# An adjacency-masked attention layer on one core: the first two graphs by rows, bias squares later, one watch operation, the last store behind the flag

## The chip, the core and the metric

The kernel runs on one core of one Trainium2 chip. The core has five engines that run side by side and wait for one another through semaphores: PE (TensorE, matrix products), DVE (VectorE), ACT (ScalarE), POOL (GpSimd) and SP (SyncE, which here only issues transfers). Data lie in HBM, on the chip in SBUF (128 partitions), and the results of PE in eight PSUM banks. The metric is the device time of one execution in microseconds (us); lower is better.

## The reference

128 graphs of 128 nodes with 768 features go through one layer: normalisation of every row, Relu, projections to queries, keys and values, attention in 12 heads of 64 with a bias and a mask from the adjacency matrix, and the sum with the input.

```python
h = jnp.maximum(_layernorm(x, axis=-1), 0.0)
q = _split_heads(h @ Wq + bq)
k = _split_heads(h @ Wk + bk)
v = _split_heads(h @ Wv + bv)
scores = jnp.einsum('bhqd,bhkd->bhqk', q, k) / jnp.sqrt(jnp.asarray(HD, x.dtype))
scores = scores + beta * adj[:, None, :, :]
scores = jnp.where(adj[:, None, :, :] > 0, scores, -9000000000000000.0)
probs = jax.nn.softmax(scores, axis=-1)
out = jnp.einsum('bhqk,bhkd->bhqd', probs, v)
return x + out.transpose(0, 2, 1, 3).reshape(B, N, D)
```

All is float32.

## The kernel before

The graphs are taken in 32 groups of four. A group's activations are held transposed, features on the partitions, as six tiles A00 to A12: A{r}{k} holds feature part k (of three) of the two graphs of half r. The products with the weights are done in three slices, `qk0`, `v` and `qk1` (the two halves of query and key columns, and the values). In most slices 18 block products are replaced by the 15 of the table `PRODUCTS`, over sums of activations (`SUMS_A`, tiles S) and of weight blocks (`SUMS_B`, tiles T). `product` (L313 on) issues the matmuls of one of them at L331, and its results are added up by ACT (L352, the first use) and DVE (L342, L347, L356). The exception is slice `qk0` of group 0: `plain_slice` takes the 18 products as they are, at L481, because the sums are not ready at the start. Its steps are counted 0 to 17, in order of r, then j (output block), then k.

The order in which things are issued is written by hand: a slice runs through its products, and behind product n it issues what the dictionary `todo` has under n (`then(n, f)`). A scheduler then places every engine's instructions in a fixed order; `tc.issue_after(i)` keeps an instruction behind another.

The start of before, for group 0. `load_x` brings each graph in four pieces of 32 rows, laid out in blocks (partition a * 32 + i holds features 192 a to 192 a + 191 of rows i, 32 + i and so on), on SP's and ACT's queues in turn. DVE takes the statistics of each block (`stats`, L227). A row's moments lie in four partitions, so PE adds them with the small matrix `mean8` (`moments_1`, L238, and `moments_2`, L254); DVE finishes them (L241 to L259), POOL raises to the power -0.5 (L261) and makes the shift (L263), ACT normalises with Relu (`norm`, L272), and DVE transposes in 32x32 blocks (`to_hT`, L279). `half(0, step)` does this for graphs 0 and 1, `half(1, step)` for graphs 2 and 3, whose moments are issued behind steps 1 and 2 of the plain slice. Ten matmuls on the identity (L530) stand behind the square matmuls of the moments, to keep PE at work. The other groups' rows are prepared in the same way during the group before, in slice v.

Attention of one output block is `scores` (L377, then DVE at L381 and ACT's exponential at L384) and `attend` (L410): products with the values, which carry a column of ones so that column HD holds the sum of the weights. `weigh` (L387 on) bounds that sum from below (L389), takes the reciprocal (L391), multiplies (L393 on DVE, L396 on ACT in group 0) and folds both the sums and the reciprocals into the running maximum `seen`, in two operations (L399). The last blocks of the last group are taken in halves, `scores_half` and `attend_half`, whose multiply, addition (L452) and store (L454) follow each other.

The adjacency bias is prepared by `bias_1` (transposed at L298, mask at L300, scaled and capped at L301, merged into `biasT` at L304); its square is taken by ACT at L305, and `bias_2` folds the largest into `seen_b` (L310, L311).

At the end DVE takes the maximum of `seen` and `seen_b` (L628, L629), tests them (L631, L632), PE adds the tests over the partitions (L634), and DVE writes the flag `bad` (L636, L637). Every engine loads the flag (L57); if it is set, the loop `general` does the whole work again in a slower and safer way (L58). With the inputs of the reference it isn't set.

SP's queue holds nearly all transfers in one order. A transfer takes one of eight slots, and one that finds its slot in use waits for the landing of the transfer before it there.

Of the kernel before, what the change touches and what calls it, by code (L numbers as in the profile page):

```python
# [10 lines left out]
F32 = mybir.dt.float32  # L11
# [85 lines left out]
HOME = {"B00": "T12", "B10": "T10", "B02": "T0", "B20": "T4", "B11": "T13"}  # L97
SLICES = ("qk0", "v", "qk1")
# [3 lines left out]
AV_AT = (5, 8, 11)  # L102

# [8 lines left out]
def direct(ctx, tc, x, adj, wq, bq, wk, bk, wv, bv, beta, out, bad):  # L112
# [41 lines left out]
    for g in range(GRP):  # L154
        load_x(0, g, (nc.sync, nc.scalar))
    ident = const.tile([P, P], F32, name="ident")
    make_identity(nc, ident)


    fold = const.tile([P, SQ], F32, name="fold")  # L160
    nc.vector.tensor_reduce(fold, ident.rearrange("p (a i) -> p i a", i=SQ), AX.X, ALU.add)
    mean8 = const.tile([P, NB, SQ], F32, name="mean8")
    made = nc.vector.tensor_scalar(mean8, fold[:, None, :].to_broadcast([P, NB, SQ]), -0.125, None, op0=ALU.mult)
# [5 lines left out]
    seen = const.tile([P, 2, 2 * GRP], F32, name="seen")  # L169
    nc.gpsimd.memset(seen, 0.0)  # L170
    seen_b = const.tile([P, GRP], F32, name="seen_b")
    nc.gpsimd.memset(seen_b, 0.0)
    vring = [const.tile([P, 2 * GRP, VE], F32, name=f"v{i}") for i in range(7)]
    for v in vring:
        nc.gpsimd.memset(v[:, :, HD:VE], 1.0)
# [16 lines left out]
    def load_weights(sl):  # L192
        for b in [f"B{k}{j}" for j in range(3) for k in range(3)]:
            t = const.tile([P, 2, H2], F32, name=f"{sl}_{HOME.get(b, b)}")
            load_block(sl, int(b[1]), int(b[2]), t)
            wt[sl, b] = t
# [12 lines left out]
    load_weights("qk0")  # L209
    beta_c = const.tile([P, 1], F32, name="beta_c")  # L210
    nc.scalar.dma_start(beta_c, beta[None, :].to_broadcast([P, 1]))

    nc.gpsimd.tensor_scalar(beta_c, beta_c, ISCALE, None, op0=ALU.mult)
# [34 lines left out]
    squares = {}  # L248

    def moments_2(G, lo, hi, mean, d):  # L250

        n = hi - lo
        for q in range(0, P, HD):
            squares[0] = nc.tensor.matmul(pm[G, lo][q:q + HD, 1], mean8.rearrange("p a i -> p (a i)")[:, q:q + HD],  # L254
                                          d, start=True, stop=True)
# [40 lines left out]
    def bias_1(G, raw):  # L296
# [8 lines left out]
        nc.scalar.activation(a, a, AF.Square)  # L305
        return a

    def bias_2(G, a):
        bm = stat.tile([P, GRP], F32, tag="bm", name=f"bm_{G}", bufs=1)
        nc.vector.tensor_reduce(bm, a, AX.X, ALU.max)  # L310
        nc.vector.tensor_tensor(seen_b, seen_b, bm, ALU.max)  # L311
# [48 lines left out]
    es, xo, taken = {}, {}, {}  # L360
# [25 lines left out]
    def weigh(G, oc, r, pa, o):  # L386

        sm = stat.tile([P, 4, 1], F32, tag="sm", name=f"sm_{G}_{oc}_{r}")
        nc.vector.tensor_scalar(sm, pa[:, :, HD:VE], TINY, None, op0=ALU.max)  # L389
        rs = stat.tile([P, 4, 1], F32, tag="rs", name=f"rs_{G}_{oc}_{r}")  # L390
        nc.vector.reciprocal(rs, sm)  # L391
        if G:
            nc.vector.tensor_mul(o, pa[:, :, 0:HD], rs.to_broadcast([P, 4, HD]))  # L393
        else:
            for b in range(4):
                nc.scalar.activation(o[:, b], pa[:, b, 0:HD], AF.Copy, scale=rs[:, b])  # L396
        for i, t in enumerate((sm, rs)):
            s = seen[:, i, 4 * r:4 * r + 4]
            nc.vector.tensor_tensor(s, s, t.rearrange("p b e -> p (b e)"), ALU.max)  # L399

    def attend(G, oc):
        o = work.tile([P, 2, 4, HD], F32, tag="o", name=f"o_{G}_{oc}", bufs=2)
        for r in range(2):
# [8 lines left out]
            weigh(G, oc, r, pa, o[:, r])  # L412
# [26 lines left out]
    def attend_half(G, oc, r):  # L439
# [9 lines left out]
        weigh(G, oc, r, pa, o)  # L449
        give(bank)  # L450
        t = xo[G, oc, r]
        nc.vector.tensor_add(t, t, o.rearrange("p (b j) d -> p b (j d)", j=2))  # L452
        g0 = G * GRP + 2 * r
        nc.sync.dma_start(out[g0:g0 + 2, :, oc * P:(oc + 1) * P].rearrange("g n d -> n g d"), t)  # L454
# [15 lines left out]
    def plain_slice(G, sl, todo):  # L470

        n = 0
        for r in range(2):
            for j in range(3):
                bank = take()
                p = bank.rearrange("p (i w) -> p i w", i=2)
                for k in range(3):
                    a, b = A[G, f"A{r}{k}"], wt[sl, f"B{k}{j}"]
                    for i in range(2):
                        for c in range(2):  # L480
                            nc.tensor.matmul(p[:, i, :], b[:, c, i * P:(i + 1) * P], a[:, c, :],  # L481
                                             start=(k == 0 and i == 0 and c == 0), stop=(c == 1),
                                             skip_group_check=True)
# [13 lines left out]
    load_weights("v")  # L497

# [269 lines left out]
```

## Time and profile before

| | us |
|---|---|
| median of 6 runs | 2901.37 |
| lowest and highest | 2899.60 and 2901.92 |
| the profiled execution | 2902.34 |
| its span, first to last instruction | 2900.1 |

| stage of group 0 and the end, by PE's lines | start, us |
|---|---|
| warm-up matmuls, L530 | 9.51 |
| plain slice, L481 | 15.84 |
| slice v, L331 | 50.9 |
| first scores, L377 | 81.4 |
| second scores, L377 | 115.9 |
| last flag operation, L637 | 2894.89 |

"Busy" is the time in which an engine had an instruction in work; PE's instructions overlap, so its records are longer than the distance from one to the next. A float32 matmul shows as two records. A line such as L481 is that of the kernel's text above; an arrow `a<-b` names the tile that is written and those that are read, without numbers. The chain of waits is followed back from the last instruction to what released it. Idle time of an engine that isn't on that chain costs nothing by itself.

### The profile page before, as it was taken

The page shows a single profiled execution, that of the slowest core. Times are in us where ns is not written, and L with a number is a line of the kernel's source. Part 1 is how long each engine was busy: PE and PEld are TensorE (multiplying, and loading weights), DVE is VectorE, ACT ScalarE, POOL GpSimd, SP SyncE. Part 2 cuts the span into 40 slices and gives each one's busy share as a digit, 9 for nine tenths or more (in the row PEclk, how much of TensorE's full clock was granted, in tenths as well). Part 3 has the DMA queues.
Part 4 walks back from the last instruction along what each step waited for, and adds up shares of the span by engine and source line. Part 5 has one row for each costly group of instructions (what it writes and reads, how often), then busy time and mean ns, then how long its engine had stood idle before and what let it go on. Part 6 is the DMA issues. An engine that isn't in the chain of part 4 may idle for free.

```text
span 2900.1 us, 81826 instructions
## 1 busy us (share of the span) xinstructions
PE 2880.3 (99%) x35526; PEld 2017.6 (70%) x35526; DVE 1985.1 (68%) x5143; ACT 804.7 (28%) x1751; POOL 375.7 (13%) x307
## 2 busy tenths in 40 slices
PE   8999999999999999999999999999999999999998
PEld 6666677667776666766667666677676677666766
DVE  6976677766676766776667676667766677666765
ACT  1432322323222222223232232322323222322221
POOL 1111111111111111111111111111111111111110
PEclk9999999999999999999999999999999999999999
DMA  6312122121222111221112212122221222111211
GB/s 162 76 53 57 41 67 71 53 61 37 63 71 60 56 44 54 71 63 52 52 46 70 71 49 59 42 63 70 56 60 39 59 71 63 52 49 45 67 42 39
DMA packets 358621, 172.21 MB, mean 59 GB/s; under 512 B 84464, under 2 KB 358128, under 8 KB 358256
## 3 DMA queue, kind: packets, MB, share of 16 engines
q1 hardware_dynamic: 355392, 166.14, 20.9%
q8 instruction: 280, 4.59, 0.6%
q10 hardware_dynamic: 2864, 0.79, 0.1%
q14 instruction: 85, 0.70, 0.1%
HBM read 116.53 MB, written 50.33 MB: 58 GB/s over the span
## 4 chain that ended last, share of the span: by engine, by line
PE 97%; DVE 1%; issue 1%; DMA 0%; POOL 0%; ACT 0%; ACTq 0%; SPq 0%; DVEq 0%; POOLq 0%
PE bank L331 83%; PE bank L377 6%; PE bank L410 6%; PE bank L481 1%; DMA x<-in_x_dram 0%; DVE A L279 0%; DVE qk L356 0%; DVE S L285 0%; POOL rstd L261 0%; DVE e L381 0%; PE bank L238 0%; PE bank L254 0%; ACT x L272 0%; DVE qk_T L207 0%; PE bank L430 0%
## 5 line engine op out<-in xcount | busy, mean ns | idle before, releaser
L331 PE MATMUL bank<-S,qk_T 128*64 128x256 f32 x7056 | 822.6, 380 | 0.5 <-DVE qk L356 0.5
L331 PEld LDWEIGHTS bank<-S,qk_T 128*64 128x64 f32 x7056 | 502.5, 137 | 257.7 <-ACT e L384 3.8
L356 DVE TENSOR_TENSOR qk<-qk,bank 128x512 f32<-128x512 f32 x630 | 429.3, 682 | 344.2 <-PE bank L331 344.0
L352 ACT ACTIVATE qk<-bank,bqk 128x256 f32<-128x256 f32 x756 | 313.0, 471 | 1020.7 <-PE bank L331 769.8
L331 PE MATMUL bank<-S,qk_B 128*64 128x256 f32 x4032 | 478.2, 379 | 1.2 <-DVE qk L356 0.9
L331 PE MATMUL bank<-A,qk_T 128*64 128x256 f32 x4032 | 478.5, 379 | 0.4 <-DVE qk L356 0.4
L415 POOL TENSOR_TENSOR xo<-xo,o 128x512 f32<-128x512 f32 x189 | 255.9, 1354 | 1601.0 <-DVE o L393 872.1
L347 DVE TENSOR_TENSOR v<-v,bank 128x512 f32<-128x512 f32 x320 | 220.2, 688 | 296.9 <-PE bank L331 296.8
L331 PE MATMUL bank<-v_T,S 128*64 128x256 f32 x3584 | 422.7, 380 | 0.0
L384 ACT ACTIVATE e<-e 128x512 f32<-128x512 f32 x378 | 227.6, 632 | 651.0 <-DVE e L381 650.3
L331 PEld LDWEIGHTS bank<-A,qk_T 128*64 128x64 f32 x4032 | 283.6, 137 | 137.6 <-DVE qk L356 0.5
L331 PEld LDWEIGHTS bank<-S,qk_B 128*64 128x64 f32 x4032 | 278.0, 137 | 129.7 <-DVE qk L356 1.4
L331 PEld LDWEIGHTS bank<-v_T,S 128*64 128x64 f32 x3584 | 252.2, 137 | 126.4 <-issue 5.7
L272 ACT ACTIVATE x<-x,shift,rstd 128x192 f32<-128x192 f32 x512 | 228.2, 536 | 344.0 <-POOL shift L263 344.0
L381 DVE SCALAR_TENSOR_TENSOR e<-bank,biasT 128x512 f32<-128x512 f32 x378 | 231.6, 682 | 20.5 <-PE bank L377 20.1
L331 PE MATMUL bank<-v_B,S 128*64 128x256 f32 x2048 | 244.7, 380 | 0.0
L331 PE MATMUL bank<-v_T,A 128*64 128x256 f32 x2048 | 238.3, 379 | 0.0
L410 PEld LDWEIGHTS bank<-v,e 128*64 128x64 f32 x6048 | 208.6, 138 | 27.4
L279 DVE STREAM_TRANSPOSE A<-x 128x256 f32<-128x256 f32 x384 | 215.3, 611 | 7.5 <-ACT x L272 7.4
L342 DVE TENSOR_TENSOR v<-bv_b,bank 128x512 f32<-128x512 f32 x192 | 131.9, 687 | 114.2 <-PE bank L331 114.2
L410 PE MATMUL bank<-v,e 128*64 128x65 f32 x6048 | 208.2, 221 | 0.0
L331 PEld LDWEIGHTS bank<-v_T,A 128*64 128x64 f32 x2048 | 147.4, 137 | 73.9
(80 smaller groups left out, 1743.4 us busy)
## 6 DMA issues: line engine op xcount, KB each, us to landing
x<-in_x_dram SPq DMA_DIRECT2D x504, 96.0 KB, 2.4
xo<-in_x_dram SPq DMA_DIRECT2D x189, 256.0 KB, 2.8
out_dram<-xo SPq DMA_DIRECT2D x189, 256.0 KB, 2.2
adj<-in_adj_dram SPq DMA_DIRECT2D x128, 64.0 KB, 2.3
qk_T<-in_L_gnn_Wq_dram SPq DMA_DIRECT2D x10, 128.0 KB, 3.0
qk_T<-in_L_gnn_Wk_dram SPq DMA_DIRECT2D x10, 128.0 KB, 3.1
v_T<-in_L_gnn_Wv_dram SPq DMA_DIRECT2D x5, 256.0 KB, 5.8
qk_B<-in_L_gnn_Wq_dram SPq DMA_DIRECT2D x8, 128.0 KB, 3.2
```

The costliest lines, as they stand in the source:

```text
L272: nc.scalar.activation(t, t, AF.Relu, bias=shift[G, n], scale=rstd[G, n])
L279: last = nc.vector.transpose(t[:, :, g * N:(g + 1) * N].rearrange("p c (b i) -> p c b i", i=SQ), src)
L331: nc.tensor.matmul(p[q:q + HD, i, :], lhs[:, q:q + HD], rhs, start=(first and i == 0 and c == 0), stop=(c == 1), skip_group_check=True)
L342: added[G] = nc.vector.tensor_tensor(o4, bias[:, None, :, :].to_broadcast([P, 2, 4, HD]), p.rearrange("p g (h d) -> p g h d", d=HD), ALU.a ...
L347: added[G] = nc.vector.tensor_tensor(o, o, got, ALU.add if sign > 0 else ALU.subtract)
L352: nc.scalar.activation(t[:, i, :], p[:, i, :], AF.Identity, bias=bqk[:, i, oc:oc + 1], scale=float(sign))
L356: added[G] = nc.vector.tensor_tensor(t, t, p, ALU.add if sign > 0 else ALU.subtract)
L377: nc.tensor.matmul(ps[oc, i][k:k + HD, g * N:(g + 1) * N], t[r, 1, at][:, k:k + HD], t[r, 0, at], start=True, stop=True)
L381: taken[0] = nc.vector.scalar_tensor_tensor(e, ps[oc, i].rearrange("p (g n) -> p g n", g=GRP), SCORE_CAP * ISCALE, biasT[G], op0=ALU.min, ...
L384: nc.scalar.activation(e, e, AF.Exp, scale=1.0 / ISCALE)
L410: nc.tensor.matmul(pa[q:q + HD, 2 * g + i, :], es[G, oc, i][:, 2 * r + g, q:q + HD], vt[G, "v", r, h // 4][:, 4 * g + h % 4, :], start=Tru ...
L415: nc.gpsimd.tensor_add(t, t, o.rearrange("p a (b j) d -> p (a b) (j d)", j=2))
```

## The change

Graphs 0 and 1 are loaded by rows, a node on each partition, in two transfers of 64 rows each. `rows_1` takes the statistics of a whole row (two halves of 384), DVE adds epsilon and POOL takes the power. `rows_2` subtracts the mean and scales on DVE, PE transposes 128x128 blocks into PSUM, and ACT applies Relu on the way to A00, A01 and A02. 18 warm-up matmuls stand first on PE. The first bank of the plain slice is done in two halves of 128 columns, graph 0's and then graph 1's, with `second` between them. The weights of j = 0 are loaded ahead of graphs 2 and 3, and the weights of v and qk1 in the order in which they are summed. ACT's table is loaded by an operation of its own (`tables`). The moments of graphs 2 and 3 are issued behind steps 3 and 4 instead of 1 and 2, those of group 1 behind product 5 of slice v instead of 6.

The square of the first group's bias is issued behind product 5 of the next slice instead of at the end of `bias_1`, and `bias_2` behind product 9 instead of 5; all squares are scaled so that one limit serves all. `weigh` keeps sums and reciprocals side by side and folds both into `seen` in one operation, ahead of the multiply. The flag is one test and one reduction, and the multiply, addition and store of the last block are issued behind the test.

```diff
+AS_SUMMED = ("B01", "B12", "B02", "B22", "B10", "B00", "B21", "B20", "B11")
+WARM = 18
...
-    for g in range(GRP):
-        load_x(0, g, (nc.sync, nc.scalar))
+    for g in range(2):
+        t = xg[0, g] = work.tile([P, NB, QD], F32, tag="x", name=f"x_0_{g}")
+        for h, engine in enumerate((nc.sync, nc.scalar)):
+            rows = slice(h * HD, (h + 1) * HD)
+            engine.dma_start(t[rows].rearrange("p b f -> p (b f)"), x[g, rows])
...
-    load_weights("qk0")
+    load_weights("qk0", ["B00", "B10", "B20"])
+    for g in range(2, GRP):
+        load_x(0, g, (nc.sync,))
+    load_weights("qk0", [f"B{k}{j}" for j in range(1, 3) for k in range(3)])
+
+    tables = const.tile([P, 1], F32, name="tables")
+    loaded = nc.scalar.activation(tables, nhalf, AF.Relu)
...
-        nc.scalar.activation(a, a, AF.Square)
+        if G:
+            square(a)
         return a
+
+    def square(a):
+        nc.scalar.activation(a, a, AF.Square, scale=1.0005 * math.sqrt(SUM_CAP) / (BIAS_CAP * ISCALE))
...
-        nc.vector.tensor_tensor(seen_b, seen_b, bm, ALU.max)
+        nc.vector.tensor_tensor(seen[:, 16:20], seen[:, 16:20], bm, ALU.max)
...
-        sm = stat.tile([P, 4, 1], F32, tag="sm", name=f"sm_{G}_{oc}_{r}")
-        nc.vector.tensor_scalar(sm, pa[:, :, HD:VE], TINY, None, op0=ALU.max)
-        rs = stat.tile([P, 4, 1], F32, tag="rs", name=f"rs_{G}_{oc}_{r}")
-        nc.vector.reciprocal(rs, sm)
-        if G:
-            nc.vector.tensor_mul(o, pa[:, :, 0:HD], rs.to_broadcast([P, 4, HD]))
-        else:
-            for b in range(4):
-                nc.scalar.activation(o[:, b], pa[:, b, 0:HD], AF.Copy, scale=rs[:, b])
-        for i, t in enumerate((sm, rs)):
-            s = seen[:, i, 4 * r:4 * r + 4]
-            nc.vector.tensor_tensor(s, s, t.rearrange("p b e -> p (b e)"), ALU.max)
+        t = stat.tile([P, 2, 4], F32, tag="sm", name=f"sm_{G}_{oc}_{r}")
+        nc.vector.tensor_scalar(t[:, 0], pa[:, :, HD], TINY, None, op0=ALU.max)
+        nc.vector.reciprocal(t[:, 1], t[:, 0])
+        s = seen[:, 8 * r:8 * r + 8]
+        nc.vector.tensor_tensor(s, s, t.rearrange("p i b -> p (i b)"), ALU.max)
+
+        def divide():
+            if G:
+                nc.vector.tensor_mul(o, pa[:, :, 0:HD], t[:, 1, :, None].to_broadcast([P, 4, HD]))
+            else:
+                for b in range(4):
+                    nc.scalar.activation(o[:, b], pa[:, b, 0:HD], AF.Copy, scale=t[:, 1, b:b + 1])
+
+        return divide
...
-        weigh(G, oc, r, pa, o)
-        give(bank)
-        t = xo[G, oc, r]
-        nc.vector.tensor_add(t, t, o.rearrange("p (b j) d -> p b (j d)", j=2))
-        g0 = G * GRP + 2 * r
-        nc.sync.dma_start(out[g0:g0 + 2, :, oc * P:(oc + 1) * P].rearrange("g n d -> n g d"), t)
+        divide = weigh(G, oc, r, pa, o)
+
+        def store():
+            divide()
+            give(bank)
+            t = xo[G, oc, r]
+            nc.vector.tensor_add(t, t, o.rearrange("p (b j) d -> p b (j d)", j=2))
+            g0 = G * GRP + 2 * r
+            nc.sync.dma_start(out[g0:g0 + 2, :, oc * P:(oc + 1) * P].rearrange("g n d -> n g d"), t)
+
+        if r == 1 and oc == 4:
+            stores.append(store)
+        else:
+            store()
...
+                parts = (slice(0, N), slice(N, H2)) if r == j == 0 else (slice(0, H2),)
+                for at, k in [(at, k) for at in parts for k in range(3)]:
...
+                    if at is not parts[-1]:
+                        if k == 2:
+                            with tc.issue_after(last.ins):
+                                second()
+                        continue
...
+    def rows_1(g):
+
+        t = xg[0, g].rearrange("p b f -> p (b f)")
+        s = stat.tile([P, 2, nc.vector.BN_STATS_DIM], F32, tag="strow", name=f"strow_{g}", bufs=2)
+        for h in range(2):
+            with ExitStack() as behind:
+                if g:
+                    behind.enter_context(tc.issue_after(first["ve"].ins))
+                nc.vector.bn_stats(s[:, h, :], t[:, h * VH:(h + 1) * VH])
+        mv = stat.tile([P, nc.vector.BN_AGGR_DIM], F32, tag="mvrow", name=f"mvrow_{g}", bufs=2)
+        nc.vector.bn_aggr(mv, s)
+        ve = stat.tile([P, 1], F32, tag="verow", name=f"verow_{g}", bufs=2)
+        first["ve"] = nc.vector.tensor_scalar(ve, mv[:, 1:2], EPS, None, op0=ALU.add)
+        r = stat.tile([P, 1], F32, tag="rsrow", name=f"rsrow_{g}", bufs=2)
+        nc.gpsimd.tensor_tensor(r, ve, nhalf, ALU.pow)
+        return mv, r
+
+    def rows_2(g, mv, r):
+
+        v = xg[0, g].rearrange("p b (j c) -> p c (b j)", c=NC)
+        for k in range(3):
+            n = work.tile([P, 2, P], F32, tag="e", name=f"rows_{g}_{k}", bufs=6)
+            first["dve"] = nc.vector.tensor_scalar(n, v[:, 2 * k:2 * k + 2], mv[:, 0:1], r, op0=ALU.subtract,
+                                                   op1=ALU.mult)
+            bank = take()
+            p = bank[:, 0:H2].rearrange("p (c i) -> p c i", c=2)
+            for c in range(2):
+                nc.tensor.transpose(p[:, c, :], n[:, c, :], ident)
+            name = f"A0{k}"
+            if not g:
+                A[0, name] = work.tile([P, 2, H2], F32, tag=name, name=f"{name}_0", bufs=1 + (k > 0))
+            t = A[0, name][:, :, g * N:(g + 1) * N]
+            nc.scalar.activation(t, p, AF.Relu)
+            give(bank)
+
+    warm = take()
+    for n in range(WARM):
+        nc.tensor.matmul(warm[:, 0:P], ident, ident, start=True, stop=True)
+    give(warm)
+    got = [rows_1(g) for g in range(2)]
+    rows_2(0, *got[0])
+
+    def second():
+
+        rows_2(1, *got[1])
+
+        nc.gpsimd.tensor_scalar(beta_c, beta_c, ISCALE, None, op0=ALU.mult)
+        fold = const.tile([P, SQ], F32, name="fold")
+        nc.vector.tensor_reduce(fold, ident.rearrange("p (a i) -> p i a", i=SQ), AX.X, ALU.add)
+        nc.vector.tensor_scalar(mean8, fold[:, None, :].to_broadcast([P, NB, SQ]), -0.125, None, op0=ALU.mult)
+        for v in vring:
+            nc.gpsimd.memset(v[:, :, HD:VE], 1.0)
...
-            with tc.issue_after(first["dve"].ins):
-                half(1, 0)
-            then(1, lambda: half(1, 1))
-            then(2, lambda: half(1, 2))
+            then(0, lambda: behind_rows(half, 0))
+            then(3, lambda: half(1))
+            then(4, lambda: half(2))
...
-            at = 3 if G else 6
+            at = 3 if G else 5
...
-            then(5, lambda: behind_scores(bias_2, 0, early[0]))
+            then(5, lambda: square(early[0]))
+            then(9, lambda: behind_scores(bias_2, 0, early[0]))
...
-    worst = stat.tile([P, 3], F32, tag="worst", name="worst", bufs=1)
-    nc.vector.tensor_reduce(worst[:, 0:2], seen, AX.X, ALU.max)
-    nc.vector.tensor_reduce(worst[:, 2:3], seen_b, AX.X, ALU.max)
-    over = stat.tile([P, 3], F32, tag="over", name="over", bufs=1)
-    nc.vector.tensor_scalar(over[:, 0:2], worst[:, 0:2], SUM_CAP, None, op0=ALU.is_gt)
-    nc.vector.tensor_scalar(over[:, 2:3], worst[:, 2:3], (BIAS_CAP * ISCALE) ** 2, None, op0=ALU.is_ge)
+    over = stat.tile([P, 20], F32, tag="over", name="over", bufs=1)
+    found = nc.vector.tensor_scalar(over, seen, SUM_CAP, None, op0=ALU.is_ge)
     pf = take()
-    nc.tensor.matmul(pf[0:1, 0:3], ones, over, start=True, stop=True)
-    n_bad = stat.tile([1, 1], F32, tag="nbad", name="nbad", bufs=1)
-    nc.vector.tensor_reduce(n_bad, pf[0:1, 0:3], AX.X, ALU.max)
-    nc.vector.tensor_copy(bad, n_bad)
-
+    nc.tensor.matmul(pf[0:1, 0:20], ones, over, start=True, stop=True)
+    nc.vector.tensor_reduce(bad, pf[0:1, 0:20], AX.X, ALU.max)
+    with tc.issue_after(found.ins):
+        for f in stores:
+            f()
```

## The prediction

> **What bounds the kernel now.** I read the page's busy rows first, then the chain that ended last, then who PE waited for, then the order of time at both ends.
>
> ```profile
> PE 2880.3 (99%) x35526; PEld 2017.6 (70%) x35526; DVE 1985.1 (68%) x5143; ACT 804.7 (28%) x1751; POOL 375.7 (13%) x307
> PE 97%; DVE 1%; issue 1%; DMA 0%; POOL 0%; ACT 0%; ACTq 0%; SPq 0%; DVEq 0%; POOLq 0%
> ```
>
> PE is the bound: it carries 97% of the chain. The table of PE's waits totals about 14 us, nearly all before 16 us, between 98 and 111 us, and after 2890 us. From 110.5 to 2888.0 us the table by stretches has PE busy for 2777.41 of 2777.50 us. The order of PE's instructions after graph group 0 is the same in both kernels, so the middle stands still and the change is worth what it moves at the two ends. The chain from the start, pieces of time in us:
>
> ```profile
> 2.16 4.39 DMA x<-in_x_dram
> ...
> 6.74 1.15 DVE st L227 x4
> ...
> 9.83 1.05 POOL rstd L261
> ...
> 12.84 2.29 ACT x L272 x5
> 15.13 0.02 issue
> 15.16 0.63 DVE A L279
> 15.79 0.04 issue
> 15.84 6.68 PE bank L481 x16
> 22.52 0.23 PE bank L238 x4
> 22.74 1.92 PE bank L481 x8
> ```
>
> The reader sees one thread through five engines before PE's first useful matmul at 15.84, and then two paces: 16 records in 6.68 us (0.42 each), later 8 in 1.92 with neighbours overlapping (start to start 1.73, so 0.216 each). PE ran at half pace until about 21.9 us. The clock row reads full throughout and doesn't show it; the pace does. In the order of time the ten warm-up matmuls of before:
>
> ```profile
> 9.51 4.64 PE L530 MATMUL bank<-ident 128*128 128x128 f32 x20
> ```
>
> They ran slow as well (0.214 per record), ended at 14.15, and PE then sat for 1.68 us. The end:
>
> ```profile
> 2893.75 0.39 DVE xo L452
> 2894.14 0.09 DVE worst L628
> 2894.23 0.02 issue
> 2894.26 0.18 DVE over L631
> 2894.44 0.04 issue
> 2894.48 0.20 PE bank L634 x2
> 2894.68 0.02 issue
> 2894.71 0.16 DVE nbad L636
> 2894.87 0.02 issue
> 2894.89 0.14 DVE bad L637
> ```
>
> The flag stands at 2895.03 and the span ends at 2900.1. In SP's waits of that tail the longest (2.1 us) is for PE's branch at L58, which comes after PE has read the flag. The last store's landing isn't in that list.
>
> **Part 1, the start.** The chain through moments, square matmuls, ACT normalisation and DVE transposes of graphs 0 and 1 goes; bn_stats, aggregate, pow, three DVE scalings, six PE transposes and three ACT Relu copies per graph take its place. Step by step, in us from the span's start:
>
> - Warm-ups no longer wait for the statistics, only for the identity, which DVE's first operation saw at 2.17. There are 18, or 36 records. All slow they end at 2.2 + 36 x 0.214 = 9.9. In the trace 4.6 us of them and a pause did not raise the pace, and 6.0 us without a pause (15.84 to 21.9) did; I take 5.3, so 25 slow records to 7.5 and 11 at 0.108: **8.7**, bounds 8.4 to 9.9.
> - Graph 0 was complete for DVE at 4.66, graph 1 at 6.74, each in four pieces of 96 KB beside two graphs more. Now each is two pieces, and nothing but weights follows: I take 4.3 and 5.6, and 6.7 as the late end for graph 1.
> - DVE: statistics of 192 elements took 1.14 for four; two of 384 cost about 1.0; aggregate and epsilon 0.2 each (the 0.17 rows). POOL's pow took 1.05 for 4 columns and 1.64 for 8, a line that gives 0.6 for one. Graph 0's scale is ready at 6.4, but graph 1's statistics stand ahead on DVE until 7.1. Three scalings of 256 elements (0.33 each, by L434; 0.2 if they run like L301's 0.48 for 512) end at 8.1, or 9.2 with the late graph. So the warm-ups, not the data, release the first transposes.
> - A PE transpose was never traced. Below lies a 65-column record pair (0.06), above a slow 128-column one (2 x 0.214). I take two fast 128-column records, 0.216, as the nearest form: six cost 1.3. ACT's copies (0.47, L352) lie beside them. Useful matmuls begin at 8.7 + 1.3 = **10.0** in place of 15.84.
> - From there to the v slice: 48 half-width records at 0.108 = 5.2, graph 1's transposes 1.3, 15 steps of 1.73 = 25.9, two moment matmuls 0.5: 32.9. The v slice starts at **42.9**; before it was 50.9. Gain 8.0, of which 3.3 is pace (16 records at 0.42 against 0.216).
>
> The Trainium skill speaks against this. "TensorE: Matmul & The Clock Gate", section "Part 4: PE-mode transpose", says that transposes do not count as PE work for the clock and take about 0.275 us each in a kernel; by it six would cost 1.65, and the start would gain 7.3 rather than 8.0. No transpose of this trace can show it. Its section "What's actually happening" puts the rise after one full free-running window of 3.4 us, which for a start at 2.2 would be an estimated 5.6 to 9.0 and warm-ups that end at 7.8 to 9.6.
>
> What this moves. SP's weights for j = 0 are issued ahead of graphs 2 and 3; a DMA here took 2.4 to 3.2 from issue to landing, and the sixth weight waits for the first one's slot: about 9, needed at 12. Statistics of graphs 2 and 3 go from steps 1 and 2 to 3 and 4: PE reaches step 4's matmul at 10.0 + 6.5 + 3.7 = 20.2 + 0.1. Before, from that matmul (24.60) to A10 of graph 3 (31.70) took 7.1; so A10 is there at 27.4 and PE wants it at 27.3. What was 3 us of slack is none: I charge **0.3**, up to 1.5. DVE's 26 sums at 0.60 then end at 43.9, each ahead of its product; the v weights, before on SP until 26 and landed by 32, are wanted from 30. Beta's scaling, `fold` and `mean8` (0.2, 0.4, 0.2) move behind graph 1's scalings, where DVE next waits for graph 2; in the way they would cost 0.6.
>
> **Part 2, group 0's tail.** In before DVE idled 3.5 at 49.4 to 52.9; that cover is gone, so group 1's statistics, pow (3.2) and 16 normalisations (0.44 each) end some 3 later relative to PE. On ACT two pairs of evictions (0.8 each) stand behind them, and PE's third qk1 product waits for the first pair: about 1.5. The bias squares (0.62) leave that spot. Against this stand 1.9 us that PE lost to DVE between 81.4 and 110.5 (27.17 busy of 29.1): DVE is full there from its first score at 82.6, so a late PE finds its banks free. Net **0**, between 1.5 lost and 1.9 gained.
>
> **Part 3, one watch operation.** 192 pairs of it become one each: DVE saves about 0.07 x 384, hidden in 32% idle. But it now waits for the reciprocal, and the multiply queues behind it: 0.06 later. In the last 5 us DVE is the chain, with some four of these: **-0.2**, from nothing to -0.4.
>
> **Part 4, the end.** The flag no longer waits for multiply and add (L393 to L452, 2893.26 to 2894.14), the maximum (L628) and the cast (L637). Watch 2893.27, test 2893.46 to 2893.63, matmul to 2893.87, reduction behind the multiply on DVE to about 2894.1: **0.95** earlier than 2895.03. The store is issued near 2894.5, 0.3 later; SP reads the flag behind it and is free at 2895.4, and with 2 us the data land at 2896.6, under PE's branch (now until 2898.1). If that cover were gone, the end would be later by the store's 0.3 only.
>
> Sum: 8.0 - 0.3 + 0 - 0.2 + 0.95 = **8.4** off a span of 2900.1. The profiled run took 2902.34, 2.24 around its span and 0.97 over the median of 2901.37; I subtract from the median: **2893.0**.
>
> **Rivals.** *The start gives back (0.13):* graph data land late or the pace rises late (start at 11.5 to 12.5), and A10 stalls 1.5. For it: the first 10 us have DMA at 0.93 busy; against: PE's need for bytes is the same order as before. Gain 8.4 - 2 - 1.2 = 5.2 or down to 3: 2896.2 to 2898.4.
> *The gain is hidden (0.06):* DVE's full stretch to 110.5 sets the time, and DVE's own start moved only by 4.6 (its transposes end at about 28.1, before 32.75). For it: 27.91 busy of 29.1 us. Against: DVE idled 7 us before that. If also the slack is eaten by the new ACT order, 1.5 and 2 more go: about 1.8 gain, 2899.6.
> *Slower (0.06):* the multiply that frees an attention bank now stands behind a watch that waits. If in the steady state PE came to that bank first, 0.1 for each of 372 pairs would be 37 us: 2930. It decides only if the 0.06 exceed the lead with which DVE frees banks; DVE waited 335 us for PE at L356, and PE lost 0.1 in 2777, which speaks against it.
>
> **How the numbers follow.** Forecast 0.75. Its own range is 2890.8 (pace early, DVE's 1.9 won) to 2895.4. The range of 2890.3 to 2897.3 takes in most of the first rival. A measurement tells 0.2%, 5.8 us, from nothing: under 2895.6. Faster 0.79, same 0.15, slower 0.06.
>
> **What would show it.** First plain matmul near 10.0 at 0.108 a record; v slice near 42.9; no PE wait over 1 us at the step to r = 1; PE waiting on ACT after the first scores, with the gaps near 105 to 110 gone; flag 5 us before the end, the store's landing not waited for. Wrong, if warm-ups run slow past 9.9, if graph 0 reaches DVE after 5.5, or if PE waits appear after group 0.

## The result, and the profile after

| | before | after |
|---|---|---|
| median, us | 2901.46 (38 runs) | 2894.38 (18 runs) |
| lowest and highest | 2899.51 and 2903.78 | 2893.26 and 2895.30 |
| profiled execution, and its span | 2902.34, 2900.1 | 2894.44, 2892.3 |

The ratio is 0.9976, with a 95% interval of 0.9970 to 0.9983: some 7 us faster, where 8.4 were forecast. The page's busy row and chain for the changed kernel:

```profile
PE 2879.6 (100%) x35562; PEld 2020.4 (70%) x35562; DVE 1962.3 (68%) x4743; ACT 801.5 (28%) x1750; POOL 371.1 (13%) x304
PE 97%; issue 1%; DVE 1%; DMA 0%; POOL 0%; ACT 0%; SPq 0%; ACTq 0%; POOLq 0%; DVEq 0%
```

PE's busy time is nearly what it was (2880.3), and its idle time fell from 19.8 to 12.7, so most of the gain is idle time. Records at half pace count as busy; fewer of them are left, and more warm-ups and the transposes stand in their place. DVE has 23 us less to do; what that is worth, experiment 4 tells. The start, by the chain of waits (start, length, what):

```profile
2.01 5.21 DMA qk_T<-in_L_gnn_Wq_dram
7.21 0.02 issue
7.23 2.34 DMA qk_T<-in_L_gnn_Wk_dram
9.57 0.42 PE bank L549 x2
10.00 2.68 PE bank L498 x24
12.68 0.66 PE bank L549 x6
13.33 0.04 issue
13.37 4.67 PE bank L498 x32
```

and PE's matmuls there in order of time (start, length, and in brackets the wait ahead of them):

```profile
2.15 6.42 PE L560 MATMUL bank<-ident 128*128 128x128 f32 x36 [2.15 <-POOL ident masks.py:199]
8.70 1.30 PE L549 MATMUL bank<-ident,rows 128*128 128x128 f32 x6
9.83 2.84 PE L498 MATMUL bank<-A,qk_T 128*128 128x128 f32 x24
12.51 0.82 PE L549 MATMUL bank<-ident,rows 128*128 128x128 f32 x6
```

The thread through five engines is gone. The chain names two weight transfers ahead of the transposes (L549) at 9.57, but that link is only inferred and can't be what set the start: the transposes read no weights, and the transfer issued at 7.23 landed 3.4 us later, at 10.66, with weights that are first read near 11.6 (16 records of 0.112 behind 9.83). What the transposes of graph 0 waited for is told by DVE's scalings and by the transposes' weight loads (PEld):

```profile
8.14 2.80 DVE L544 TENSOR_SCALAR rows<-x,mvrow,rsrow 128x256 f32<-128x256 f32 x6
8.70 0.20 PEld L549 LDWEIGHTS bank<-ident,rows 128*128 128x128 f32 x2 [0.32 <-DVE rows L544]
9.12 0.20 PEld L549 LDWEIGHTS bank<-ident,rows 128*128 128x128 f32 x2 [0.22 <-DVE rows L544]
9.55 0.20 PEld L549 LDWEIGHTS bank<-ident,rows 128*128 128x128 f32 x2 [0.23 <-DVE rows L544]
```

Each pair of transposes waits for its scaling. The 24 half-width records run start to start at 0.112 and not at twice that: full pace from the first. Before, 16 full-width records took 6.68 us.

| PE reaches | before | after | gain |
|---|---|---|---|
| slice v | 50.92 | 43.00 | 7.92 |
| first scores | 81.39 | 73.25 | 8.14 |
| second scores | 115.87 | 108.09 | 7.78 |
| sixth scores | 294.73 | 286.89 | 7.84 |
| last scores | 2829.97 | 2822.73 | 7.24 |
| flag written | 2895.03 | 2886.93 | 8.10 |
| end of the span | 2900.11 | 2892.28 | 7.83 |

The 0.6 between the sixth and the last scores is scatter: in the fourteen profiles of this study that stretch took from 2535.1 to 2536.4, in no order that goes with an edit. The end of the chain:

```profile
2886.09 0.18 DVE seen L397
2886.26 0.02 issue
2886.29 0.18 DVE over L696
2886.46 0.33 DVE o L401
2886.79 0.04 DVE bad L699
```

The test (L696) follows the watch (L397) at once. The multiply and the addition for the store no longer stand ahead of the test.

### The profile page after: what moved, and what is told of

It is laid out like the page before. It is cut to its first block, busy times and chain, and to the rows that moved or that the text cites. A ratio compares the mean times of both kernels' runs of the same rounds, so it can differ in the third digit from the quotient of the medians.

```text
span 2892.3 us, 81358 instructions
## 1 busy us (share of the span) xinstructions
PE 2879.6 (100%) x35562; PEld 2020.4 (70%) x35562; DVE 1962.3 (68%) x4743; ACT 801.5 (28%) x1750; POOL 371.1 (13%) x304
## 4 chain that ended last, share of the span: by engine, by line
PE 97%; issue 1%; DVE 1%; DMA 0%; POOL 0%; ACT 0%; SPq 0%; ACTq 0%; POOLq 0%; DVEq 0%
PE bank L336 84%; PE bank L417 6%; PE bank L382 6%; PE bank L498 1%; ACT x L273 0%; POOL rstd L262 0%; DMA qk_T<-in_L_gnn_Wq_dram 0%; DMA x<-in_x_dram 0%; DVE S L286 0%; DVE qk L361 0%; PE bank L241 0%; PE bank L255 0%; PE bank L437 0%; DMA qk_T<-in_L_gnn_Wk_dram 0%; DVE qk_T L206 0%
## 5 line engine op out<-in xcount | busy, mean ns | idle before, releaser
L357 ACT ACTIVATE qk<-bank,bqk 128x256 f32<-128x256 f32 x756 | 311.5, 471 | 1009.3 <-PE bank L336 778.1
L230 DVE BATCH_NORM_STATS2 st<-x 128x6 f32<-128x192 f32 x504 | 154.6, 345 | 76.3 <-DMA x<-in_x_dram 76.0
```

The source lines that it names most:

```text
L230: nc.vector.bn_stats(st[G][:, g * NB + b, :], xg[G, g][:, b, :])
L357: nc.scalar.activation(t[:, i, :], p[:, i, :], AF.Identity, bias=bqk[:, i, oc:oc + 1], scale=float(sign))
```

## The experiments

Each time is a median, and each kernel was timed beside the kernel before on the same chip: the first four beside 2901.37, the next four beside 2900.65, three more beside 2901.46, the last beside 2901.00. The kernel before differs by up to 0.8 between these groups, so a difference of that size between kernels of two groups says little. The two columns on the right are from the profiles (43.00 and 108.09 in the changed kernel).

| kernel | us | ratio to before, interval | slice v | second scores |
|---|---|---|---|---|
| no warm-ups | 2901.77 | 1.0002, 0.9993 to 1.0011 | 44.87 | 115.50 |
| 10 warm-ups | 2896.73 | 0.9985, 0.9976 to 0.9994 | 44.06 | 110.93 |
| end alone | 2899.97 | 0.9993, 0.9984 to 1.0002 | 49.42 | 114.15 |
| watch twice | 2894.21 | 0.9974, 0.9963 to 0.9984 | 42.84 | 107.46 |
| moments a step later | 2894.36 | 0.9977, 0.9968 to 0.9986 | 43.00 | 108.08 |
| squares early | 2894.07 | 0.9976, 0.9967 to 0.9985 | 43.08 | 107.63 |
| sums on POOL | 2895.22 | 0.9981, 0.9972 to 0.9990 | 44.49 | 109.09 |
| graph 0 first | 2894.68 | 0.9980, 0.9971 to 0.9989 | 42.21 | 108.91 |
| no warm-ups, copies first | 2896.43 | 0.9983, 0.9974 to 0.9992 | 43.97 | 109.30 |
| graph 0 first, bias late | 2893.32 | 0.9973, 0.9964 to 0.9983 | 42.22 | 107.54 |
| before, 16 warm-ups | 2899.86 | 0.9996, 0.9987 to 1.0005 | 47.89 | 112.84 |
| ... and sums later too | 2892.60 | 0.9972, 0.9960 to 0.9983 | 42.31 | 106.50 |

**1. Without warm-ups.**

```diff
-    for n in range(WARM):
-        nc.tensor.matmul(warm[:, 0:P], ident, ident, start=True, stop=True)
```

> The changed kernel without its 18 warm-up matmuls; all else stays. In the changed kernel the pace doubles 6.67 us after the span's start, 4.5 us after the first warm-up. Theory (some 4.5 us of matmul work without a long pause raise the pace, and transposes count as such work): the first transposes come at about 8.5, the pace doubles at about 13 to 13.5, and what ran until then cost twice as much: the v slice starts 2 to 2.4 us later than 43.00, time about 2896.5. Rival 1 (the short waits between the first steps start the count anew, or transposes don't count): the pace doubles at 15 or later, the v slice starts 3 us later or more, about 2897.5. Rival 2 (the pace doesn't matter, the weights' arrival at 9.6 sets the start): v slice within 0.5 us of 43.00, about 2894.5.

The whole gain was gone. Up to slice v the loss is 1.87, a little under the theory, and the pace doubled at 13.45, as it says. But 5.5 more were lost from there to the second scores, which no theory had. PE's waits from 20 to 130 us in this run (total, times, longest), then in the changed kernel:

```profile
PE bank L336 <- ACT qk L357: 5.4, 1, 5.4
PE bank L336 <- DVE qk L361: 0.4, 1, 0.4
```

```profile
PE bank L336 <- DVE qk L361: 1.9, 2, 1.0
PE bank L336 <- ACT qk L357: 0.8, 1, 0.8
```

ACT's operations there in order of time, without warm-ups and then in the changed kernel:

```profile
75.69 7.12 ACT L273 ACTIVATE x<-x,shift,rstd 128x192 f32<-128x192 f32 x16 [5.08 <-POOL shift L264]
82.71 1.53 ACT L357 ACTIVATE qk<-bank,bqk 128x256 f32<-128x256 f32 x4
```

```profile
68.98 7.12 ACT L273 ACTIVATE x<-x,shift,rstd 128x192 f32<-128x192 f32 x16 [25.03 <-POOL shift L264]
76.01 1.53 ACT L357 ACTIVATE qk<-bank,bqk 128x256 f32<-128x256 f32 x4
```

The 16 normalisations of group 1 stand ahead of the copies (L357) that PE waits for, and here they start 6.7 later: the scheduler put DVE's statistics of group 1, and so the matmuls of its moments, later in the order (67.21 against 61.34), though the missing warm-ups are the only edit. The wait of 5.37 then slowed PE itself. The same run by stretches (PE's busy time first, the granted clock third from the end):

```profile
75.00:80.00 5.00, 3.21 (x99) 2.61 (x96) 3.43 (x6) 4.31 (x10) 0.57 (x2) 1.00 0.00 2
80.00:85.00 5.00, 1.42 (x8) 0.85 (x10) 4.52 (x9) 5.00 (x13) 0.00 (x0) 0.67 0.00 0
85.00:90.00 5.00, 5.00 (x34) 2.94 (x32) 0.20 (x1) 3.15 (x7) 0.00 (x0) 0.65 0.01 3
90.00:95.00 5.00, 5.00 (x74) 3.57 (x72) 5.00 (x10) 1.68 (x4) 0.00 (x0) 1.00 0.43 115
```

The clock fell to one half at 81.72 and rose again 6.83 later. Of the 5.5, 4.6 are the longer wait, 2.4 the half pace (32 records in 6.10, in the changed kernel in 3.67), and 1.5 came back where PE waited less for DVE.

**2. Ten warm-ups**, `WARM = 10`.

> The changed kernel with 10 warm-ups, as many as the kernel before had, in place of 18. They run from 2.15 to about 6.4, then PE has nothing until about 8.6. Theory (a pause of 2 us makes the count start anew): like no warm-ups, the pace doubles at about 13 and the v slice starts 2 to 2.4 us later than 43.00, time about 2896.5. Rival 1 (work before the pause still counts): pace doubles before 10, loss under 0.7, about 2895. Rival 2 (fixed stretches of time, not PE's work, decide): the pace doubles at a time that no warm-up count changes, near 6.7, so loss 0.

The time is what the theory gave, but not for its reason. By stretches:

```profile
5.00:7.00 2.00, 1.08 (x9) 0.89 (x7) 1.73 (x5) 0.00 (x0) 0.47 (x1) 1.00 1.13 219
7.00:9.00 2.00, 0.50 (x3) 0.32 (x4) 1.93 (x7) 0.00 (x0) 0.90 (x3) 0.90 1.28 173
9.00:11.00 2.00, 2.00 (x11) 1.86 (x11) 2.00 (x5) 1.15 (x3) 1.13 (x2) 0.50 1.11 234
11.00:13.00 2.00, 2.00 (x15) 2.00 (x15) 0.98 (x5) 0.00 (x0) 0.00 (x0) 0.74 1.09 213
```

The pace doubled at 5.19, 3.04 after the first warm-up, halved at 8.61 after the pause, and doubled again at 12.02. Slice v came 1.06 later; the rest is a wait of 2.64 for ACT in the tail, with half pace from 80.29 to 83.70. So neither a count of work nor a count that starts anew decides; how it goes is shown in the last section.

**3. The end alone**: the kernel before with `weigh`, the flag and the last store of the changed one.

> The kernel before with the one watch operation and the flag ahead of the last store; the start stays as before. Theory: from the last score matmuls to the end of the span it wins 0.6 to 0.95 us, and the steady stretch is as before; span about 2899.3, time about 2900.6. Rival 1 (the last store's landing sets the end): no gain, 2901.4. Rival 2 (the watch that waits for the reciprocal holds up the banks): a loss over the steady stretch of 1 us or more.

The time can't be told from before by its interval. The trace tells more: from the last scores to the flag 64.19 us, before 65.06, after 64.20. That is the 0.86 of the changed kernel. Then the span goes on for 5.61 (before 5.07, after 5.35), so from the last scores to the end of the span 0.33 was won, less than the theory gave. In all twelve profiles with the new end that rest was 5.32 to 5.75, in the two with the old one 5.06 and 5.07: of the 0.86 at the flag, 0.25 to 0.7 is lost behind it.

It is lost in PE's branch at L58, for which SP waits last. The branch starts 0.63 to 0.64 behind the flag in all fourteen profiles and takes 3.38 and 3.39 with the old end, 3.63 to 3.99 with the new one. Why it takes longer there wasn't tried. The last store landed 2.4 ahead of the branch's end here (2894.42 against 2896.79), which speaks against rival 1, and the stretch from the sixth to the last scores took 2535.1 (before 2535.2), which speaks against rival 2. The earlier slice v of this run (49.42 against 50.92) goes with the pace, which rose earlier than in the profile before: see the last section.

**4. The watch doubled.**

```diff
-        nc.vector.tensor_tensor(s, s, t.rearrange("p i b -> p (i b)"), ALU.max)
+        for i in range(2):
+            nc.vector.tensor_tensor(s[:, 4 * i:4 * i + 4], s[:, 4 * i:4 * i + 4], t[:, i], ALU.max)
```

> The changed kernel with two watch operations in the one's place, ahead of the same multiply: the cost of the watch doubled. Theory: DVE gets about 384 x 0.15 = 58 us more work, hidden under PE in the steady stretch; in the last 5 us four of these stand in the chain, 0.2 to 0.5 us later; time 2894.5 to 2894.9. Rival (the multiply behind the watch frees the banks that PE waits for): up to 0.15 for each of some 370, so anything from 5 to 56 us more.

Twice the operations, no time: PE waited 0.4 in all between 116 and 2860 us, in the changed kernel 0.3. But the edit did not double the watch's cost. DVE's busy time grew by 14 us (1976.5 against 1962.3) and not by 58, and at the end it took 0.23 from the reciprocal to the test in both, so the 0.2 to 0.5 there didn't come (from the last scores to the flag 64.18, in the changed kernel 64.20). The rival that made the watch hold up the banks falls by the 0.3 of waits in the changed kernel itself; and that halving the watch was worth anything is shown nowhere.

**5. Moments a step later**, `at = 6` for group 0 as in before.

> The changed kernel with group 1's moments and normalisations one step later in the v slice, as the kernel before had them. It does the same work. In the changed kernel PE waits 0.77 for ACT's eviction at 76.87, behind 13 normalisations. Theory (those normalisations stand ahead of the eviction): placed a step later, more of them follow behind it or it waits more; the gap becomes 0.5 to 1.5 us, and the second scores, 108.09, move by at most 0.8 to either side; time 2894 to 2895. Rival (the stretch is bound by DVE, which waits for the normalisations): transposes come late, second scores 1 to 2 us later, 2895.5.

Nothing moved: the same gap of 0.77, second scores at 108.08. The order of PE and of ACT's first 120 operations was that of the changed kernel. The step in `todo` did not move these matmuls; what places them wasn't tried. So the run says nothing on either theory.

**6. The squares early**, at the end of `bias_1` for group 0 too, with `bias_2` at 5.

> The changed kernel with the bias squares of group 0 right behind the bias, as before, and their maximum at step 5 again. Theory: ACT's 0.62 us of squares stand ahead of the evictions that PE waits for near 76 to 78; the gap of 0.77 there grows to about 1.3, of which the later DVE waits (0.93 and 1.0 at 98 and 101) give most back: time within 0.3 of 2894.4. Rival (each us that ACT is late is a us of the whole): 0.6 later, 2895.

As the theory said: the gap for ACT grew to 1.29, the gaps for DVE shrank from 1.93 to 1.08, and the time stayed. This part of the change brought nothing by itself: without it the second scores came, if anything, 0.46 earlier.

**7. Four sums on POOL.**

```diff
-                then(n + 2, lambda n=n: behind_scores(sum_weights, "qk0", n))
+                then(n + 2, lambda n=n: behind_scores(sum_weights, "qk0", n, nc.gpsimd if n in (1, 2, 4, 6) else None))
```

> The changed kernel with four sums of weights (0.68 each on DVE) of group 0's qk1 slice done by POOL instead. It does the same work. Theory (DVE, busy all the time from 80 to 110, makes PE wait 0.93 at 98.08 and 1.0 at 101.04): DVE has 2.7 us less to do there, both gaps go, the second scores come 1.5 to 1.9 earlier than 108.09, time about 2892.6. Rival 1 (the wait moves to POOL: sums of about 1.3 us each come too late for the products that use them, or POOL's work slows DVE's): gain under 0.5 or a loss. Rival 2 (the time regained is lost before 120, since DVE is still busy there): gain 0.5 to 1 at the end of the span.

A miss. POOL in order of time:

```profile
19.26 1.26 POOL L206 TENSOR_TENSOR qk_T<-qk_B,qk_T 128x512 f32<-128x512 f32 x1 [8.93 <-DMA qk_B<-in_L_gnn_Wk_dram]
21.20 1.27 POOL L206 TENSOR_TENSOR qk_T<-qk_T,qk_B 128x512 f32<-128x512 f32 x1 [0.69 <-DMA qk_B<-in_L_gnn_Wk_dram]
22.43 1.68 POOL L262 TENSOR_TENSOR rstd<-ve,nhalf 128x8 f32<-128x8 f32 x1
```

Two sums stood 60 us ahead of where they were meant, in front of the power for graphs 2 and 3 (22.43, in the changed kernel 20.93). That came 1.5 later, and PE waited 1.29 for A10 at the step to r = 1. So the slack there is 0.2 us.

The theory missed as well. With four sums fewer on DVE the two gaps went from 1.93 to 1.37, not to nothing, and from slice v to the second scores 0.49 was gained (64.60 against 65.09) where 1.5 to 1.9 were given. In this order DVE's work on group 1's bias, from 103.15 on in the changed kernel, begins at 94.87, ahead of both gaps (99.67 and 101.96).

**8. Graph 0 first.**

```diff
-WARM = 18
+WARM = 14
...
-    got = [rows_1(g) for g in range(2)]
+    got = [rows_1(0)]
     rows_2(0, *got[0])
+    got.append(rows_1(1))
```

> The changed kernel with graph 1's statistics behind graph 0's scalings on DVE, not ahead of them, and 14 warm-ups. It does the same work. Theory (with graph 1's statistics out of the way graph 0's scalings start at 7.4 and not 8.14; 28 warm-up records end at 7.5): plain matmuls start at about 9.0, but graph 1's scalings now end 1.7 later, near 12.6, so its first matmuls come at about 13.0 to 13.4: gain 0 to 0.4 at the v slice. Rival 1 (the weights of k = 2, landing near 9.6 or later, hold PE): no gain. Rival 2 (14 warm-ups aren't enough for the pace): loss of 1.5 us or more.

The plain matmuls came at 9.05 and slice v 0.79 earlier, more than the theory gave. DVE and the warm-ups were both moved here; that DVE was the later one in the changed kernel is told by its trace (above), where the last warm-up ended at 8.57 and the first scaling at 8.64. The second scores came 0.82 later all the same. The scheduler had again moved group 1's moments back (62.34 against 61.34, with slice v earlier), PE waited 2.2 for ACT at 77.8, and the clock was at one half from 79.14 to 82.55.

**9. No warm-ups, and the copies first on ACT.** `norm(1, g)` is issued behind the copies of qk1's product 1 and no longer in slice v:

```diff
+            for g in range(GRP):
+                todo[1].insert(g, lambda g=g: behind_evictions(norm, 1, g))
```

> The changed kernel without warm-ups, and with group 1's normalisations on ACT behind the copies of qk1's first two products. The run without warm-ups alone lost 7.4 us: 1.87 up to the v slice, and in the tail of group 0 a wait of 5.37 for ACT's copies, with PE at half pace from 81.7 to 88.5. Theory (the late loss comes from the place of group 1's normalisations ahead of the copies, and the half pace from the pause that this makes): with the copies first there is no wait over 1.3 us and no half pace after the start; the loss against the changed kernel is that of the start, some 1.5 to 2.5: about 2896.3. Rival (the late loss comes from the slow start itself: DVE is behind, and PE must wait there for whatever it is): the 5 us turn up as waits for DVE, time 2900 or more.

2896.43 against 2896.3 expected. ACT in order of time:

```profile
72.85 0.84 ACT L357 ACTIVATE qk<-bank,bqk 128x256 f32<-128x256 f32 x2 [3.13 <-PE bank L336]
74.57 0.84 ACT L357 ACTIVATE qk<-bank,bqk 128x256 f32<-128x256 f32 x2 [0.89 <-PE bank L336]
75.30 7.12 ACT L273 ACTIVATE x<-x,shift,rstd 128x192 f32<-128x192 f32 x16
```

PE's longest gap was 1.01, and no half pace was seen after the start. The late loss came from the order on ACT. What the warm-ups are worth by themselves is the start's: 0.97 at slice v, 1.21 at the second scores, 1.41 between the spans and 2.05 between the medians.

**10. Graph 0 first, the normalisations of two graphs behind the copies, group 1's bias in the next slice.** The edit of the bias, beside those of experiments 8 and 9:

```diff
-            then(13, lambda: early.append(behind_scores(bias_1, 1, load_adj(1))))
...
+                then(6, lambda: early.append(behind_scores(bias_1, 1, load_adj(1))))
```

> The changed kernel with graph 0's scalings ahead of graph 1's statistics and 14 warm-ups, with the normalisations of group 1's graphs 2 and 3 behind the copies of qk1's first two products on ACT, and with group 1's bias (3.3 us on DVE between 103 and 107) made in the next slice. It does the same work. Theory (the tail of group 0 is bound by ACT's order and then by DVE): v slice at 42.2, no wait for ACT at 76, no half pace there, and 3.3 us less for DVE before the second scores: these come at 104.8 to 106 in place of 108.09, and nothing of it is lost later: time 2891 to 2892.5. Rival 1 (the bias is missed in the next slice, or DVE is full there as well): half of it is lost again by 175, about 2893. Rival 2 (14 warm-ups or the order bring another pause and half pace): 2894.5 or more.

Faster than the changed kernel by 1.1, but less than the theory gave. Experiment 8's half pace and the wait at 76 were gone (0.26 was left, at 90), yet PE waited for DVE for 1.26 and 1.01 at 97.5 and 100.5: the bias lay behind these waits, at 103, and could not shorten them. The time is near the 2893 of rival 1, but not for its reason: nothing was lost later (31.64 from the second to the third scores in both).

**11. The kernel before with 16 warm-ups.**

> The kernel before with 16 warm-ups in place of 10, nothing else. They start at about 9.5; all at the slow pace they would end at 16.3, and if the pace doubles at 13 they end at 14.8; the first useful matmul was at 15.84. Theory (the pause of 1.7 to 2 us between warm-ups and first use costs the pace): the pace has doubled before the first useful matmul or soon after, 16 records take 3.5 or less in place of 6.68, the v slice comes 2 to 3.3 us earlier than 50.92, and time is 1 to 2.5 us under the kernel before, 2899 to 2900.3. Rival 1 (a doubled pace only moves the waits for DVE between 100 and 110): v slice earlier, time as before. Rival 2 (the warm-ups themselves come in the way): 0.5 later.

The theory held but for a detail (16 records took 3.72, not 3.5 or less): the pace doubled at 13.11, the pause was 0.75, slice v came 3.03 earlier and the time fell by 1.6, with an interval that touches no change. The waits for DVE stayed (0.35, 0.94 and 0.46 in both) and the second scores came 3.03 earlier too, which speaks against rival 1. Its 11 runs lie within 1.25 us, those of the kernel before beside it within 3.3.

**12. The tenth with less on DVE ahead of 97**: sums 6 to 8 of qk0 and `bias_2` of group 0 in the next slice.

> The run before it (graph 0 first, two normalisations behind the copies, group 1's bias later), and besides two sums of weights (0.6 each) and the maximum of group 0's bias squares (0.75 in two operations) moved from before 100 us into the next slice. It does the same work. In the run before it PE still waited for DVE, 1.26 at 97.5 and 1.01 at 100.5, because the bias that was moved lay behind these waits and not ahead of them. Theory (DVE's work ahead of 97 sets these waits): with 2 us less ahead of them the two waits shrink from 2.3 to 0.3 to 0.6 together, the second scores come at 105.6 to 106 in place of 107.54; DVE has 5 us idle between 125 and 140 for what was moved; time 2891.3 to 2892. Rival (what is moved is missed between 110 and 130, where DVE is full): the gain is lost again by the third scores, 2893 or more.

PE's waits from 20 to 200 us:

```profile
PE bank L336 <- DVE qk L361: 1.3, 1, 1.3
PE bank L336 <- ACT qk L357: 0.3, 1, 0.3
```

The second of the two waits went, the first stayed, and the theory doesn't say why: the second scores came at 106.50 and not by 106, and the time is above its range. Nothing was lost again by the third scores (31.63). At 2892.60 this is the fastest version; its seven runs (2892.01 to 2893.04) all lie under the lowest of the changed kernel (2893.26), though the two were not run side by side.

## Why the prediction was right, point by point

- **Warm-ups** were to end at 8.7 and ended at 8.57. The rule behind the number, that 5.3 us of work raise the pace, was wrong: it rose 4.52 after the first one here, and between 3.04 and 5.5 after it in the other runs that begin with them. The bounds of 8.4 to 9.9 were made for that.
- **Data**: late. Graph 0 reached DVE at 5.13 (4.3 forecast, 4.66 before), graph 1 at 6.77, which was the late end.
- **DVE**: statistics 1.02, aggregate and epsilon 0.21 and 0.15, power 0.56, each as costed. The three scalings ended at 9.50 and not at 8.1. They started 1.0 late, at 8.14 behind the late graph 1 (for that the prediction had 9.2), and were mis-sized: 1.36 for the three and not 1.0. "The warm-ups, not the data, release the first transposes" is the step that failed, by little: the first transpose came at 8.70, behind the scaling, 0.13 after the last warm-up, and the next two pairs waited 0.2 each for DVE.
- **Transposes**: 1.3 for six, as forecast, but by chance. PE takes 0.109 for each, half of what I took; the 1.3 is the pace of the scalings.
- **Useful matmuls** at 9.83 (10.0), slice v at 43.00 (42.9). A10 was charged 0.3 and cost nothing; the slack that I put at none is 0.2 (experiment 7).
- **Part 2**: the wait for ACT was there, 0.77 and not 1.5. DVE's waits were not won back, 1.93 against 1.74. Net, from slice v to the second scores, 0.14 lost against 0 forecast.
- **Parts 3 and 4**: 0.86 at the flag where 0.95 less 0.2 was forecast. Behind the flag 0.28 was lost, where I had the end unchanged.
- **Sum**: 7.83 between the two spans: 7.92 at slice v, 0.14 lost up to the second scores, 0.06 won up to the sixth, 0.60 lost up to the last (scatter), 0.86 won at the flag and some 0.28 lost behind it. Between the medians it is 7.08. The pace term, 3.3, was worked out from one execution in which the pace rose late, at 21.87. That execution was 0.88 over its kernel's median, and another profile with the same start (experiment 3) reached slice v 1.5 earlier. I subtracted a gain against a late execution from the median.
- **A small sum**: warm-ups that start at 2.2 and double their pace at 9.0 end at about 9.5, not 9.6. Nothing rests on it.

Of the 7.92 at slice v some 3 could be had in the kernel before by six more warm-ups alone (experiment 11; 1.6 of the 7.08 between medians). The rest is the earlier start: the first useful matmul came 6.0 earlier (15.84 to 9.83), and 1.1 of that was spent again by slice v (33.17 from there, 32.12 in experiment 11).

Of the rivals, the one in which the start gives back was right that the data come late, but that was nearly hidden: the warm-ups ran to 8.57, and the first scaling ended at 8.64. The one in which DVE hides the gain did not come: the waits for DVE stayed at about their size and the gain passed through them. The slower one fell with experiment 4. What I had not priced is that a wait of 2 us in the tail would have cost a second time, in pace; the change stayed clear of it with 0.77.

## What to carry to other kernels

A pause of PE has two prices, the pause and the half pace that may follow, so cut the longest wait first and bridge what is left with matmuls. An edit at the start can move the scheduler's order 60 us later: compare the order of every engine, and the waits, and not only the place that was edited. Before work is taken off a full engine to end a wait, see that it lies ahead of that wait.

## What the runs showed that was not expected

**The clock goes by fixed stretches of 3.413 us.** In every trace the times between two changes of the granted clock were whole multiples of 3.413 (1, 2, 20, 21, 822, 842 to 844 of them), wherever PE's work began. Worked out from the traces, PE's busy share of the stretch that ended at a change, or that brought none:

| the clock | busy share of the stretch before |
|---|---|
| rose to full | 0.89 (10 warm-ups, to 5.19), 0.94 (experiment 9, to 11.78), 1.00 in the others |
| stayed at half | 0.84, 0.74 and 0.77 (before, 8.2 to 18.5), 0.45 (no warm-ups, from 81.7) |
| stayed full | 0.57 (experiment 10, from 96.4), 0.59 (before, from 107.2), 0.71 to 0.78 in the changed kernel's waits |
| fell to half | 0.40 (experiment 8, from 75.7; experiment 3, from 13.05), 0.29 and 0.23 (10 warm-ups), 0 (no warm-ups) |
| fell to half, at the end of the span | 0.60 (experiment 12, from 2881.06), 0.59 (experiment 10, from 2881.70), 0.06 to 0.47 in the others |

The busy share alone doesn't draw the line: 0.57 left the clock at full, and 0.60 at the end didn't. The matmuls there are attention's narrow ones (65 and 128 columns); whether that makes the difference wasn't tried.

Whether a pause near 2 us costs pace depends on where it falls in a stretch: a pause of 1.68 to 2.04 stood at the same place in both profiles of the start of before, and the pace rose at 21.87 in the one, at 13.05 in the other, to fall at 16.46 and rise for good at 19.88. That would account for the wide scatter of the kernel before (4.3 us) and the narrow one with 16 warm-ups; it was not tried in any other way.

The Trainium skill, "TensorE: Matmul & The Clock Gate", section "What's actually happening", has free-running windows of 3413 ns; these runs agree. It puts the fall after an idle window; here a stretch that was 40% busy was enough.

**Transposes seem to count as PE's work.** In experiment 9 the stretch of 8.37 to 11.78 was 0.94 busy with the six transposes and 0.55 without, and the clock rose at its end; with ten warm-ups the stretch of 8.61 to 12.02 was 1.00 and 0.64. Stretches of 0.74 to 0.84 without transposes had not raised it (table). A transpose took 0.109 from start to start at full pace (12.51 on, above) and 0.214 at half pace without warm-ups.

The same page's section "Part 4: PE-mode transpose" says that they don't count in the same way, and gives about 0.275 us each in a kernel, for bf16; those here are float32. Both runs speak against the first. The second is the length of one record here (0.273), but records overlap, and the rate is 0.109.
